# Layer 1's experts in a four-layer kernel: output pieces of 32 columns, the ranking inside the first expert, and mu loaded two tiles before its square

## The chip, the core and the metric

The kernel runs on one core of one Trainium2 chip. A core has a tensor engine (PE, with its weight loads shown apart as PEld), a vector engine (DVE), a scalar engine (ACT), a general engine (POOL) and a queue processor (SP) that issues most of the transfers between memory and the core's buffers. [...] The metric is device microseconds of one execution; the figure that counts is the median of several runs.

## The reference, cut to what matters

Four layers follow one another, each adding to the stream `x` of 32 x 64 = 2048 tokens of 512 numbers. The change lies in layer 1, a mixture of 32 experts, and in one preparation for layer 2 that is done meanwhile.

```python
# layer 1
logits = x @ gate_w.T + gate_b                    # 32 experts
topk_logits, topk_idx = top_k(logits, 4)
topk_weight = softmax(topk_logits)
order = argsort(topk_idx.reshape(-1))             # pairs of token and expert, by expert
xt = repeat(x, 4, axis=0)[order]
gate = ragged_dot(xt, w_gate, group_sizes) + b_gate[gid]
up = ragged_dot(xt, w_up, group_sizes) + b_up[gid]
gate = minimum(gate, 7); up = clip(up, -7, 7)
activated = (up + 1) * gate * sigmoid(1.702 * gate)
outs = ragged_dot(activated, w_down, group_sizes) + b_down[gid]
y = sum over a token's four outs, times topk_weight
# layer 2, the part prepared during layer 1
mu_n = mu / maximum(sqrt(sum(mu * mu, axis=0)), 1e-12)   # mu is 512 x 2048
```

## The kernel before

**Front of layer 1** (`layer1`, L1325). A loop over 16 tiles of 128 tokens adds layer 0's experts to the stream, mixes, computes the 32 logits and picks four experts per token. `put` (L845) and `placed` (L1167) give every pair of token and expert its place in the expert's list and write the token numbers into a small table `tok` of 96 x 128, a sum of products on PE. `end` (L1189) closes the front. First four small products bring the token numbers of the first two experts, which have fixed places, into a column form (`fixed`, L1192 to L1197), and a cast puts them into columns 0 to 4 of the integer table `stok` (L1198). Then comes the ranking of the other experts by load: totals (`tot`), keys, a permutation `perm`, the numbers of the ranked experts (`nth`), from which the gather addresses of their weights (`widx`) and biases (`each`) come, the lists in ranked order (`lists`, `ranked`), nine products that spread them over the 66 other tiles (L1225), a cast into the rest of `stok` (L1229), and the room of each expert (`room`, `count`). All of it stands ahead of the expert stage, and its constants, the group `cst1`, are loaded into a pool of the front (L1336).

**Expert stage** (`Moe.run`, L1011). The ranked experts have 320, 320, 352, 320 (three), 288 (15) and 256 (11) rows, end to end 9088 rows, 71 output tiles of 128. Three local functions issue the work of PE, whose order is written out by hand: `follow` (L1025) makes each PE instruction come after the one issued before it.

- `turn(t)` (L1035) transposes gathered rows `xr` of tile t and copies them to `xT`, by ACT and DVE in turn.
- `into(u, ic)` (L1050) multiplies the rows of expert u by half `ic` of its gate and up weights (`gu`, four PSUM buffers) and hands them to `l1_expert` (L712): DVE, a sigmoid on ACT into `sg`, a product on POOL (L722, kept in program order), and DVE again, into `hT`.
- `out_of(t)` (L1066) multiplies by the down weights into `y`. A tile can hold rows of two experts; `of_expert` lists its pieces (expert, column, row, count), which are at most 32 rows at row 32 or 96, at most 64 at row 64, and up to 128 at row 0. DVE adds the bias piece by piece into one of four `yo` buffers (L1079), and SP writes it out (L1082).

The loop at L1093 goes over experts and interleaves: after each of the four products of an expert comes a `turn` for the next expert and an `out_of` of the one before. POOL issues the gathers: `ready` (L891) asks for five tiles of rows right after `end`; in the first expert, `rows_to` and `weights` (L1113 to L1115) ask for tiles 5 to 7 and for the third expert's weights after the first half; later ones are asked for two experts ahead. The first two experts' weights are loaded by SP.

**Beside it.** After each `out_of`, `ahead` (L1383) is called. Every fourth of the first 16 tiles it computes slots; from tile 16 on it takes one step of the generator `layer2_ahead` (L1395): eleven loads of layer 2's weights, two steps of small work, and then, one a tile, 16 steps that each load 128 x 512 of mu (`mus`, two buffers) through SP and at once square and sum it on ACT (L1424 to L1428). A power on POOL (`cn`, L1429) and three DVE steps end it. `keep_in_program_order`, also as `pin`, holds an instruction at its place in its engine's order.

Of the kernel before, what the change touches and what calls it, by code (L numbers as in the profile page):

```python
# [47 lines left out]
CH = NK // 3  # L48


_GROUPS = ("cst", "cst01", "cst3", "cst1")


def _spread():

    sel, at = [], FIXED1 * 320 // P
    for shift in range(0, P, 32):
        for low in range(2 if shift else 1):
            s = np.zeros((P, TILES1 - at), np.float32)
            for u in range(FIXED1, E1):  # L60
                for c in range(-(-CAP1[u] // P)):
                    t = (BASE1[u] + c * P) // P + low
                    if BASE1[u] % P == shift and c * P + low * (P - shift) < CAP1[u]:
# [9 lines left out]
    s, parts = sel[0]  # L73
    odd = s * (np.arange(P)[:, None] % 2).astype(np.float32)
    return [(s - odd, parts), *sel[1:], (odd, parts)]


def _consts():
# [43 lines left out]
    d["spread"] = np.concatenate([s for s, _ in _spread()], 1)  # L122
    return dict(zip(_GROUPS, (a, b, c, d)))


def _rope_table():
# [99 lines left out]
class Prog:  # L226
# [9 lines left out]
        self.ident = self.c("ident")  # L236
        self.ones = self.c("ones")

    def constants(self, pool, group):
        t = self.load(pool, group)  # L240
# [471 lines left out]
def l1_expert(g, sb, hT, gate, up, bias):  # L712

    nc = g.nc
    ga = sb.tile([P, gate.shape[1]], F32, name="ga")
    nc.vector.tensor_scalar(ga, gate, bias[:, 0:1], 7.0, ALU.add, ALU.min)
    sg = sb.tile([P, gate.shape[1]], F32, name="sg")
    nc.scalar.activation(sg, ga, AF.Sigmoid, scale=1.702)  # L718
    up_ = sb.tile([P, gate.shape[1]], F32, name="up")
    nc.vector.tensor_scalar(up_, up, bias[:, 1:2], 7.0, ALU.add, ALU.min)  # L720
    nc.vector.tensor_scalar(up_, up_, -7.0, 1.0, ALU.max, ALU.add)
    g.pin(nc.gpsimd.tensor_tensor(ga, ga, sg, ALU.mult))  # L722
    nc.vector.tensor_tensor(hT, up_, ga, ALU.mult)  # L723


class Moe:
# [8 lines left out]
    def __init__(self, g, ctx, keep, E, K, caps, V, wname, wlen, act, scale, bias=None):  # L735
# [28 lines left out]
        for parts, sizes, whole in (  # L764
            (self.of_unit, [n for _, _, n in self.units], True), (self.of_expert, caps, False)
        ):
            at = 0
            for k, size in enumerate(sizes):
                col = 0
                while col < size:  # L770
                    row = at % P
                    n = min(size - col, P - row)
                    if not whole and row:
                        n = min(n, 64 if row == 64 else 32)
                    parts[at // P].append((k, col, row, n))
                    col, at = col + n, at + n

    def weights(self, e):
        if e < self.E and e not in self.wts:
# [118 lines left out]
    def rows_to(self, end):  # L898

        while self.asked < min(end, self.tiles):  # L900
            t = self.asked
            self.xrs[t] = self.xp.tile([P, D], F32, name="xr")
            self.g.gather(self.xrs[t], self.rows, self.stok[:, t : t + 1], later=self.ranked)
            self.asked += 1

    def beyond(self):

# [103 lines left out]
    def run(self, xs, per_tile):  # L1011
# [8 lines left out]
        with ExitStack() as ctx:  # L1020
# [45 lines left out]
            def out_of(t):  # L1066
                y = ps.tile([P, D], F32, name="y", tag="y")
                for ic in range(2):
                    for e, col, row, n in self.of_expert[t]:
                        wd = self.parts(self.weights(e))[2]  # L1070
                        follow(nc.tensor.matmul(  # L1071
                            y[row : row + n, :], hTs[e][:, ic, col : col + n], wd[:, ic, :],
# [17 lines left out]
            while turned < tiles_to(0):  # L1090
                turn(turned)
                turned += 1
            for u in range(len(self.units)):  # L1093
                k = 0
                e = self.units[u][0]
# [5 lines left out]
                for ic in range(2):  # L1101
                    for _ in into(u, ic):
                        if turned < tiles_to(u + 1):
                            turn(turned)
                            turned += 1
                        k += 1
                        if k > 1 and u and (done + 1) * P <= ends[u - 1]:
                            out_of(done)
                            done += 1
# [41 lines left out]
class Ranked(Moe):  # L1151
# [3 lines left out]
    def begin(self, sb, bank, at):  # L1155
        nc, g = self.g.nc, self.g
        self.bank, self.at = bank, at
        nc.vector.memset(self.pre[:, 0], 0.0)
        self.tok = sb.tile([TC1, P], F32, name="tokens1", bufs=1)
        nc.vector.memset(self.tok, 0.0)  # L1160
        self.number = sb.tile([32, P], F32, name="number1", bufs=1)
        nc.vector.tensor_scalar(self.number, g.ones[0:32, :], g.c("p")[0:32], None, ALU.mult)
        self.room = self.keep.tile([P, 2, E1], F32, name="room1")
        self.widx = self.keep.tile([P, E1], I32, name="widx1")
        self.each = self.keep.tile([P, E1], I32, name="each1")

    def placed(self, sb, hot, i, n):  # L1167

# [20 lines left out]
    def end(self, sb):  # L1189
# [3 lines left out]
        for o, cols, which in (  # L1193
# [1 line left out]
            (fixed[64:P, 2:5], slice(0, 64), slice(1, 96, 32)), (fixed[0:64, 3:5], slice(64, P), slice(1, 64, 32)),  # L1195
        ):
            nc.tensor.matmul(o, tok[:, cols], ident[0:TC1, which], start=True, stop=True)  # L1197
        nc.vector.tensor_copy(self.stok[:, 0:5], fixed)  # L1198

        tot = self.at[:, 0:E]  # L1200
        nc.tensor.matmul(tot, g.ones, self.pre[:, NT], start=True, stop=True)
        key = sb.tile([P, E], F32, name="key", bufs=1)
        nc.vector.tensor_tensor(key, tot, g.c("keym"), ALU.mult)
        nc.vector.tensor_tensor(key, key, g.c("keyc"), ALU.add)
        junk = sb.tile([P, E], F32, name="junk1", bufs=1)
        own = sb.tile([P, 2], F32, name="own1", bufs=1)
# [4 lines left out]
        perm = sb.tile([TC1, TC1], F32, name="perm1", bufs=1)  # L1211
        nc.vector.tensor_scalar(perm, g.c("blk")[0:TC1], own[0:TC1, 1:2], None, ALU.is_equal)
        nth = self.at[:, 32:64]
        nc.tensor.matmul(nth, self.number, perm[0:32, 0:32], start=True, stop=True)
        nc.vector.tensor_scalar(self.widx, nth, float(P), g.c("p"), ALU.mult, ALU.add)
        nc.vector.tensor_copy(self.each, nth)
        lists = self.bank[0:TC1, 256:384]
        nc.tensor.matmul(lists, perm, tok, start=True, stop=True)
        ranked = sb.tile([TC1, P], F32, name="ranked1", bufs=1)
        nc.vector.tensor_tensor(ranked, lists, g.c("within")[0:TC1], ALU.mult)  # L1220
        first, n = FIXED1 * 320 // P, self.tiles - FIXED1 * 320 // P
        table, at, k = self.bank[:, 384 : 384 + n], 0, 0
        todo = [(part, j) for j, (_, parts) in enumerate(_spread()) for part in parts]
        for k, ((to, row, rows), j) in enumerate(todo):
            nc.tensor.matmul(  # L1225
                table[to : to + rows], ranked[:, row : row + rows], g.c("spread")[0:TC1, j * n : (j + 1) * n],
                start=k == 0, stop=k == len(todo) - 1,
            )
        nc.vector.tensor_copy(self.stok[:, first:], table)  # L1229

        dg = sb.tile([32, 2, E], F32, name="dg1", bufs=1)
        for k, name in enumerate(("base1", "cap1")):
            nc.vector.scalar_tensor_tensor(
                junk[0:32], perm[0:32, 0:32], 1.0, g.c(name)[0:32], ALU.mult, ALU.mult, accum_out=own[0:32, k : k + 1]
            )
            nc.vector.tensor_scalar(dg[:, k], ident[0:32, 0:32], own[0:32, k : k + 1], None, ALU.mult)
        room = self.at[:, 64:128]
        nc.tensor.matmul(room, g.ones[0:32, :], dg.rearrange("p k e -> p (k e)"), start=True, stop=True)
# [86 lines left out]
def layer1(g, bridge, combined, beside, w2):  # L1325
    tc, nc, a = g.tc, g.nc, g.a
    with ExitStack() as ctx:
# [67 lines left out]
def layer2_ahead(g, w):  # L1395
# [25 lines left out]
    nc.vector.tensor_scalar(w["mask"], adf, g.c("pd16"), sc, ALU.is_equal, ALU.mult)  # L1421
    yield
    cs = pool.tile([P, 16], F32, name="cs2")
    for e in range(16):  # L1424
        m = sb.tile([P, D], F32, name="mus", bufs=2)
        g.dma(m, a["mu_s"][e * P : (e + 1) * P, :])
        nc.scalar.activation(m, m, AF.Square, accum_out=cs[:, e : e + 1])
# [1013 lines left out]
```

## Time and profile before

| what | us |
|---|---|
| median of 3 runs (lowest, highest) | 2646.71 (2644.03, 2647.79) |
| the profiled execution | 2657.32 |
| its span, first to last instruction | 2655.4 |
| DVE cast of the first five tiles' token numbers (L1198), start | 734.98 |
| first gather of the expert stage on POOL, start | 740.42 |
| first gu product on PE, start | 748.26 |
| last y product of the stage, start | 1179.3 |
| the 16 mu loads on SP, first and last issue | 941.9, 1045.1 |
| the 16 squares on ACT, each; first and last start | 0.63; 946.9, 1048.4 |

Times of instructions count from the start of the span. In a row of the timeline stand start, length, engine, line, operation, the tile written and those read, the shapes, a count of merged records, and in brackets how long the engine had been idle and what ended the idle time. "128*32 128x512" is a stationary operand of 128 rows and 32 columns with 512 columns streamed past it. An f32 product leaves two records. A row of the waits has the instruction that waited, what it waited for, the sum, the count and the longest.

### The profile page before, as it was taken

Reading aid. Unit: us, or ns where it says so; the run is one execution under the profiler, and the core shown is the slowest. Engines: PE = TensorE matmul, PEld = TensorE weight load, DVE = VectorE, ACT = ScalarE, POOL = GpSimd, SP = SyncE. Lnnn points to the kernel's source line nnn. Section 1 sums busy time; section 2 is a strip of 40 time slices with the busy share of each in tenths; the row PEclk is TensorE's granted clock in tenths of the full one; section 3 lists DMA queues with packets and bytes.
Section 4 is the critical chain, followed back from the end, with each engine's and each line's share of the span. In section 5 each row is a group of like instructions: output and inputs, shape, how many; then the busy total and the mean of one; then the engine's idle time right before and its main releaser. Section 6 shows DMA issues by size and latency. Waiting matters only on the chain.

```text
span 2655.4 us, 42159 instructions
## 1 busy us (share of the span) xinstructions
PE 2479.6 (93%) x16444; PEld 1626.1 (61%) x16459; DVE 1411.6 (53%) x3463; ACT 719.6 (27%) x1505; POOL 906.5 (34%) x955
## 2 busy tenths in 40 slices
PE   6999998997789999978999999999999999979998
PEld 4777775664556655756666666666666665445554
DVE  3666656653745444445554544454444432557886
ACT  2444330111311111101322222222222221246664
POOL 2222215533244434433333333333332311573440
PEclk9999998997689999999999999999999999989999
DMA  2333224456556866854222222222222313524441
GB/s 99 106 120 130 102 72 165 170 167 194 182 179 215 344 245 217 275 173 149 67 70 74 74 73 73 72 70 70 70 70 74 97 58 122 170 67 121 135 136 45
DMA packets 132421, 339.34 MB, mean 128 GB/s; under 512 B 23977, under 2 KB 24777, under 8 KB 124912
## 3 DMA queue, kind: packets, MB, share of 16 engines
q1 hardware_dynamic: 90576, 188.83, 20.7%
q0 software_dynamic: 41056, 141.89, 16.9%
q10 hardware_dynamic: 576, 5.77, 0.5%
q8 instruction: 135, 2.21, 0.3%
q14 instruction: 78, 0.64, 0.1%
HBM read 245.21 MB, written 107.22 MB: 133 GB/s over the span
## 4 chain that ended last, share of the span: by engine, by line
PE 41%; DVE 10%; issue 2%; POOL 1%; DMA 1%; ACT 0%; another core or an unknown queue 0%; ACTq 0%; POOLq 0%; SPq 0%; DVEq 0%
PE out L1814 9%; PE lp L1671 6%; PE gp L1803 3%; PE pp L2128 3%; PE zp L1748 3%; PE yp L1616 2%; PE y L2376 2%; PE hp L1780 2%; PE pT L2329 2%; PE op L2354 2%; PE sp L2307 2%; DVE xt L1145 1%; PE ep L1757 1%; DVE inv L1707 1%; PE kp L2280 1%
## 5 line engine op out<-in xcount | busy, mean ns | idle before, releaser
L1059 PE MATMUL gu<-xT,wt 128*128 128x320 f32 (+3 forms) x1472 | 398.9, 418 | 4.8 <-ACT xT L299 3.7
L1059 PEld LDWEIGHTS gu<-xT,wt 128*128 128x128 f32 x1472 | 277.5, 193 | 125.0 <-issue 52.8
L1814 PE MATMUL out<-sb_w,gT 128*128 128x512 f32 x512 | 233.5, 599 | 12.4 <-DVE nn L1651 6.6
L1671 PEld LDWEIGHTS lp<-xnT,sb_mu 128*128 128x128 f32 x2048 | 234.8, 193 | 9.2 <-issue 6.7
L1671 PE MATMUL lp<-xnT,sb_mu 128*128 128x128 f32 x2048 | 237.8, 276 | 2.1 <-DVE xnT L301 1.4
L1748 PE MATMUL zp<-sb_w,xnT 128*128 128x512 f32 x512 | 228.4, 595 | 5.6 <-DVE z L1750 5.5
L1071 PE MATMUL y<-wt,hT 128*128 128x512 f32 (+3 forms) x492 | 216.7, 596 | 2.3 <-DVE hT L723 2.3
L329 POOL DMA_INDIRECT kvst<-kv,gidx x96 | 97.0, 1010 | 280.9 <-DMA oldkv<-kvst 212.0
L1807 DVE COPY gT<-gp 128x512 f32<-128x512 f32 x64 | 44.3, 692 | 251.8 <-PE gp L1803 251.4
L1814 PEld LDWEIGHTS out<-sb_w,gT 128*128 128x128 f32 x512 | 93.2, 190 | 117.6 <-issue 95.2
L1748 PEld LDWEIGHTS zp<-sb_w,xnT 128*128 128x128 f32 x512 | 93.7, 190 | 113.4 <-issue 99.9
L329 POOL DMA_INDIRECT yk<-ys,slot x96 | 104.1, 1085 | 125.3 <-SPq L917 66.2
L329 POOL DMA_INDIRECT kvt<-newkv,oidx x96 | 99.8, 1040 | 134.9 <-DMA kvt<-oldkv 76.9
L329 POOL DMA_INDIRECT xr<-rows,stok x106 | 102.6, 968 | 81.1 <-DVE stok L1229 40.7
L1785 ACT ACTIVATE h<-hp 128x512 f32<-128x512 f32 x128 | 69.5, 595 | 218.5 <-PE hp L1780 218.3
L1071 PEld LDWEIGHTS y<-wt,hT 128*128 128x128 f32 (+3 forms) x492 | 75.4, 175 | 78.4 <-issue 62.9
L722 POOL TENSOR_TENSOR ga<-ga,sg 128x288 f32<-128x288 f32 (+3 forms) x64 | 50.5, 789 | 183.3 <-ACT sg L718 182.1
L1825 POOL TENSOR_TENSOR xt<-xt,bc_bias 128x512 f32<-128x512 f32 x16 | 20.5, 1280 | 228.5 <-DMA x<-xt 213.2
L1676 DVE TENSOR_TENSOR lT<-lp,cmu 128x512 f32<-128x512 f32 x64 | 43.5, 680 | 94.4 <-PE lp L1671 89.1
L1803 PEld LDWEIGHTS gp<-lT,h 128*64 128x64 f32 x2048 | 66.3, 140 | 38.7 <-issue 25.8
L1709 POOL TENSOR_TENSOR eT<-eT,inv 128x512 f32<-128x512 f32 x64 | 71.7, 1122 | 52.2 <-DVE inv L1708 43.9
L1079 DVE TENSOR_TENSOR yo<-y,bd 128x512 f32<-128x512 f32 (+3 forms) x88 | 60.7, 689 | 53.3 <-PE y L1071 52.0
(426 smaller groups left out, 4641.0 us busy)
## 6 DMA issues: line engine op xcount, KB each, us to landing
ys<-yo SPq DMA_DIRECT2D x106, 256.0 KB
oldkv<-kvst SPq DMA_DIRECT2D x96, 224.0 KB
kvt<-oldkv SPq DMA_DIRECT2D x96, 224.0 KB
ys<-zero SPq DMA_DIRECT2D x10, 2048.0 KB
xt<-x SPq DMA_DIRECT2D x62, 256.0 KB
x<-xt SPq DMA_DIRECT2D x48, 256.0 KB
wt<-w_e SPq DMA_DIRECT2D x7, 1536.0 KB
sb_w<-w SPq DMA_DIRECT2D x5, 1024.0 KB
```

Of the source, the lines that this page charges most:

```text
L329: ins = self.nc.gpsimd.indirect_dma_start(out=out, out_offset=None, in_=src, in_offset=bass.IndirectOffsetOnAxis(ap=idx, axis=0), **kw)
L1059: follow(nc.tensor.matmul(o, wj[:, c, ic * P : (ic + 1) * P], xTs[u][:, c, 0:n], start=c == 0, stop=c == 3))
L1071: follow(nc.tensor.matmul(y[row : row + n, :], hTs[e][:, ic, col : col + n], wd[:, ic, :], start=ic == 0, stop=ic == 1,))
L1079: nc.vector.tensor_tensor(yo[r], y[r], self.bds[e][r], ALU.add)
L1616: g.first(c, nc.tensor.matmul(yp, self.xT[:, c, :], w["w_2"][:, c, :], start=c == 0, stop=False))
L1671: g.first(e + c, nc.tensor.matmul(lp[:, e, :], w["mu"][:, c, (4 * q + e) * P : (4 * q + e + 1) * P], self.xnT[:, c, :], start=c == 0, stop ...
L1709: g.pin(nc.gpsimd.tensor_tensor(e3, e3, inv.unsqueeze(2).to_broadcast([P, 8, T]), ALU.mult))
L1748: g.first(c, nc.tensor.matmul(zp, self.xnT[:, c, :], w["w1"][:, c, cols], start=c == 0, stop=c == 3))
L1785: g.pin(nc.scalar.activation(self.hs[q][b], hp[:, b], AF.Gelu))
L1803: g.first(e + b + k, nc.tensor.matmul(gp[r, e, cols], self.hs[q][b][:, e, r], self.lT[q][:, e, cols], start=True, stop=True))
L1814: g.first(e, nc.tensor.matmul(self.out, self.gTs[q][:, e, :], w["w2"][:, 4 * q + e, :], start=q + e == 0, stop=q + e == 6 and q == 3))
L2128: nc.tensor.matmul(pp, xT[i][:, c, :], (w["w_kv3"] if z else wq)[:, c, :], start=c == 0, stop=c == 3)
```

## The change

1. `pieces` is a second list beside `of_expert`: where a tile has a piece whose count isn't a multiple of 64, all its pieces are cut into pieces of 32 rows. `out_of` multiplies by `pieces`; the bias is still added by `of_expert`.
2. `end` keeps the fixed products alone, and their cast goes into a table of its own, `fixed`. The ranking is the generator `rank`, in three parts, run by `next(ranking)` after the first expert's transposes and after its first and second product. Its constants are two groups now, `cst1` and `cst1s`, loaded by SP into `yo` buffers of the expert stage; a third `yo` buffer and one `y` bank are its working space. The even and odd split of the spreading products is gone (eight products), and one product with zeros (`none`) ends the sum, so nine remain.
3. The mu loop takes 18 iterations: the square of iteration e is of the load of iteration e - 2, and the first 16 iterations take two steps each.
4. `sg` in the experts' form has two buffers, not three.

```diff
@@ constants
+    def constants(self, pool, group, **kw):
+        if kw:
+            n = self.a[group].shape[1]
+            t = pool.tile([P, D], F32, **kw)
+            self.dma(t[:, 0:n], self.a[group], later=False)
+        else:
+            t = self.load(pool, group)
@@ l1_expert
-    sg = sb.tile([P, gate.shape[1]], F32, name="sg")
+    sg = sb.tile([P, gate.shape[1]], F32, name="sg", **(dict(bufs=2) if gate.shape[1] > P else {}))
@@ Moe
+        self.pieces = [
+            parts if all(n % 64 == 0 for *_, n in parts) else
+            [(e, col + k, row + k, 32) for e, col, row, n in parts for k in range(0, n, 32)]
+            for parts in self.of_expert
+        ]
...
-            self.g.gather(self.xrs[t], self.rows, self.stok[:, t : t + 1], later=self.ranked)
+            self.g.gather(self.xrs[t], self.rows, self.tokens_of(t), later=self.ranked)
@@ run
-                    for e, col, row, n in self.of_expert[t]:
+                    for e, col, row, n in self.pieces[t]:
...
+            ranking = self.rank(sb, ps, follow)
+            next(ranking, None)
             for u in range(len(self.units)):
...
                             turn(turned)
                             turned += 1
                         k += 1
+                        next(ranking, None)
                         if k > 1 and u and (done + 1) * P <= ends[u - 1]:
@@ Ranked
+        self.fixed = self.keep.tile([P, FIXED1 * 320 // P], I32, name="fixed1")
+
+    def tokens_of(self, t):
+        n = FIXED1 * 320 // P
+        return self.fixed[:, t : t + 1] if t < n else self.stok[:, t - n : t - n + 1]
...
-        nc.vector.tensor_copy(self.stok[:, 0:5], fixed)
...
+        nc.vector.tensor_copy(self.fixed, fixed)
+
+    def rank(self, sb, ps, follow):
+
+        g, nc, E, tok, ident = self.g, self.g.nc, self.E, self.tok, self.g.ident
+        for group in ("cst1", "cst1s"):
+            g.constants(sb, group, name="yo", bufs=4)
+        work = sb.tile([P, D], F32, name="yo", bufs=4)
...
+        follow(nc.tensor.matmul(tot, g.ones, self.pre[:, NT], start=True, stop=True))
+        g.pin(nc.vector.tensor_tensor(key, tot, g.c("keym"), ALU.mult))
         nc.vector.tensor_tensor(key, key, g.c("keyc"), ALU.add)
...
         nc.vector.tensor_scalar(perm, g.c("blk")[0:TC1], own[0:TC1, 1:2], None, ALU.is_equal)
+        nc.vector.tensor_scalar(number, g.ones[0:32, :], g.c("p")[0:32], None, ALU.mult)
+        yield
+
+        follow(nc.tensor.matmul(lists, perm, tok, start=True, stop=True))
+        follow(nc.tensor.matmul(nth, number, perm[0:32, 0:32], start=True, stop=True))
+        nc.vector.tensor_tensor(ranked, lists, g.c("within")[0:TC1], ALU.mult)
...
+        yield
+
+        todo = [(part, j) for j, (_, parts) in enumerate(_spread()) for part in parts]
+        for k, ((to, row, rows), j) in enumerate(todo):
+            follow(nc.tensor.matmul(
+                table[to : to + rows], ranked[:, row : row + rows], g.c("spread")[0:TC1, j * n : (j + 1) * n],
+                start=k == 0, stop=False,
+            ))
+        follow(nc.tensor.matmul(table, ranked, g.c("none")[0:TC1], start=False, stop=True))
+        nc.vector.tensor_copy(self.stok[:, 0:n], table)
+        follow(nc.tensor.matmul(room, g.ones[0:32, :], dg, start=True, stop=True))
         nc.vector.tensor_copy(self.room.rearrange("p k e -> p (k e)"), room)
...
@@ layer1
-            g.constants(wp, "cst1")
@@ layer2_ahead
-    for e in range(16):
-        m = sb.tile([P, D], F32, name="mus", bufs=2)
-        g.dma(m, a["mu_s"][e * P : (e + 1) * P, :])
-        nc.scalar.activation(m, m, AF.Square, accum_out=cs[:, e : e + 1])
+    mus = {}
+    for e in range(18):
+        if e >= 2:
+            m = mus.pop(e - 2)
+            nc.scalar.activation(m, m, AF.Square, accum_out=cs[:, e - 2 : e - 1])
+        if e < 16:
+            mus[e] = sb.tile([P, D], F32, name="mus", bufs=2)
+            g.dma(mus[e], a["mu_s"][e * P : (e + 1) * P, :])
         yield
+        if e < 16:
+            yield
```

More of the change, by code (lines that the diff above doesn't have):

```diff
@@ L48 @@
 CH = NK // 3
-_GROUPS = ("cst", "cst01", "cst3", "cst1")
+_GROUPS = ("cst", "cst01", "cst3", "cst1", "cst1s")
 def _spread():
@@ L72, in _spread @@
                 sel.append((s, parts))
-    s, parts = sel[0]
-    odd = s * (np.arange(P)[:, None] % 2).astype(np.float32)
-    return [(s - odd, parts), *sel[1:], (odd, parts)]
+    return sel
 def _consts():
@@ L121, in _consts @@
     d["within"] = (p[:, None] // 32 * P + p[None, :] < np.array(CAP1)[p % 32][:, None]).astype(f)
-    d["spread"] = np.concatenate([s for s, _ in _spread()], 1)
-    return dict(zip(_GROUPS, (a, b, c, d)))
+    d["none"] = np.zeros((P, TILES1 - FIXED1 * 320 // P), f)
+    s = {"spread": np.concatenate([s for s, _ in _spread()], 1)}
+    return dict(zip(_GROUPS, (a, b, c, d, s)))
 def _rope_table():
@@ L237, in __init__ @@
         self.ones = self.c("ones")
-    def constants(self, pool, group):
-        t = self.load(pool, group)
+    def constants(self, pool, group, **kw):
[5 more added lines that the diff above has]
+            t = self.load(pool, group)
         at = 0
@@ L902, in rows_to @@
             self.xrs[t] = self.xp.tile([P, D], F32, name="xr")
-            self.g.gather(self.xrs[t], self.rows, self.stok[:, t : t + 1], later=self.ranked)
+            self.g.gather(self.xrs[t], self.rows, self.tokens_of(t), later=self.ranked)
             self.asked += 1
+    def tokens_of(self, t):
+        return self.stok[:, t : t + 1]
+    def rank(self, sb, ps, follow):
+        return iter(())
     def beyond(self):
@@ L1158, in begin @@
         nc.vector.memset(self.pre[:, 0], 0.0)
-        self.tok = sb.tile([TC1, P], F32, name="tokens1", bufs=1)
+        self.tok = self.keep.tile([TC1, P], F32, name="tokens1")
         nc.vector.memset(self.tok, 0.0)
-        self.number = sb.tile([32, P], F32, name="number1", bufs=1)
-        nc.vector.tensor_scalar(self.number, g.ones[0:32, :], g.c("p")[0:32], None, ALU.mult)
         self.room = self.keep.tile([P, 2, E1], F32, name="room1")
@@ L1165, in begin, with tokens_of @@
         self.each = self.keep.tile([P, E1], I32, name="each1")
+        self.fixed = self.keep.tile([P, FIXED1 * 320 // P], I32, name="fixed1")
+    def tokens_of(self, t):
+        n = FIXED1 * 320 // P
+        return self.fixed[:, t : t + 1] if t < n else self.stok[:, t - n : t - n + 1]
     def placed(self, sb, hot, i, n):
@@ L1197, in end, with rank @@
             nc.tensor.matmul(o, tok[:, cols], ident[0:TC1, which], start=True, stop=True)
[L1198 to L1203, printed above, removed]
+        nc.vector.tensor_copy(self.fixed, fixed)
+    def rank(self, sb, ps, follow):
+        g, nc, E, tok, ident = self.g, self.g.nc, self.E, self.tok, self.g.ident
+        for group in ("cst1", "cst1s"):
+            g.constants(sb, group, name="yo", bufs=4)
+        work = sb.tile([P, D], F32, name="yo", bufs=4)
+        key, junk, own = work[:, 0:32], work[:, 32:64], work[:, 64:66]
+        perm, ranked = work[0:TC1, 96:192], work[0:TC1, 192:320]
+        dg, number = work[0:32, 320:384], work[0:32, 384:512]
+        bank = ps.tile([P, D], F32, name="y", tag="y")
+        tot, nth, room = bank[:, 0:32], bank[:, 32:64], bank[:, 64:128]
+        n = self.tiles - FIXED1 * 320 // P
+        lists, table = bank[0:TC1, 128:256], bank[:, 256 : 256 + n]
+        follow(nc.tensor.matmul(tot, g.ones, self.pre[:, NT], start=True, stop=True))
+        g.pin(nc.vector.tensor_tensor(key, tot, g.c("keym"), ALU.mult))
         nc.vector.tensor_tensor(key, key, g.c("keyc"), ALU.add)
-        junk = sb.tile([P, E], F32, name="junk1", bufs=1)
-        own = sb.tile([P, 2], F32, name="own1", bufs=1)
         nc.vector.scalar_tensor_tensor(junk, key, 1.0, g.c("same32"), ALU.mult, ALU.mult, accum_out=own[:, 0:1])
@@ L1210, in end @@
         )
-        perm = sb.tile([TC1, TC1], F32, name="perm1", bufs=1)
         nc.vector.tensor_scalar(perm, g.c("blk")[0:TC1], own[0:TC1, 1:2], None, ALU.is_equal)
-        nth = self.at[:, 32:64]
-        nc.tensor.matmul(nth, self.number, perm[0:32, 0:32], start=True, stop=True)
+        nc.vector.tensor_scalar(number, g.ones[0:32, :], g.c("p")[0:32], None, ALU.mult)
[3 more added lines that the diff above has]
+        nc.vector.tensor_tensor(ranked, lists, g.c("within")[0:TC1], ALU.mult)
         nc.vector.tensor_scalar(self.widx, nth, float(P), g.c("p"), ALU.mult, ALU.add)
         nc.vector.tensor_copy(self.each, nth)
[L1217 to L1231, printed above, removed]
         for k, name in enumerate(("base1", "cap1")):
@@ L1235, in end @@
             )
-            nc.vector.tensor_scalar(dg[:, k], ident[0:32, 0:32], own[0:32, k : k + 1], None, ALU.mult)
-        room = self.at[:, 64:128]
-        nc.tensor.matmul(room, g.ones[0:32, :], dg.rearrange("p k e -> p (k e)"), start=True, stop=True)
+            nc.vector.tensor_scalar(dg[:, 32 * k : 32 * k + 32], ident[0:32, 0:32], own[0:32, k : k + 1], None, ALU.mult)
+        yield
[8 more added lines that the diff above has]
+        follow(nc.tensor.matmul(room, g.ones[0:32, :], dg, start=True, stop=True))
         nc.vector.tensor_copy(self.room.rearrange("p k e -> p (k e)"), room)
```

## The prediction, made before the result was known

> **What bounds the kernel now.** I read the page's busy times first, then the table of engine time by stage, then the timeline of TensorE (PE) inside the stage that the change touches, and last the waits there.
>
> ```profile
> PE 2479.6 (93%) x16444; PEld 1626.1 (61%) x16459; DVE 1411.6 (53%) x3463; ACT 719.6 (27%) x1505; POOL 906.5 (34%) x955
> ```
>
> ```profile
> 690.00:770.00 80.00, 61.92 (x261) 43.25 (x262) 42.80 (x141) 18.72 (x32) 20.70 (x18) 0.65 0.46 159
> 770.00:1190.00 420.00, 402.58 (x1570) 261.56 (x1568) 197.96 (x394) 54.28 (x131) 170.17 (x183) 0.98 0.69 245
> ```
>
> The columns are stretch, length, then busy time of PE, weight loads, DVE, ACT and POOL, then granted clock, DMA share and GB/s. Layer 1's expert stage (770 to 1190) is bound by PE, 402.6 of 420.0 us. Ahead of it (690 to 770) PE has idle time and a clock of 0.65: that stretch is bound by a chain.
>
> The timeline of PE inside the stage shows what a shared tile costs:
>
> ```profile
> 778.94 1.94 PE L1071 MATMUL y<-wt,hT 128*64 128x512 f32 x8
> 780.81 2.42 PE L1059 MATMUL gu<-xT,wt 128*128 128x320 f32 x8
> 783.06 1.88 PE L1071 MATMUL y<-wt,hT 128*128 128x512 f32 x4
> 784.78 2.32 PE L1059 MATMUL gu<-xT,wt 128*128 128x320 f32 x8
> 835.55 4.00 PE L1071 MATMUL y<-wt,hT 128*96 128x512 f32 x8
> 839.48 2.42 PE L1059 MATMUL gu<-xT,wt 128*128 128x320 f32 x8
> 905.28 4.04 PE L1071 MATMUL y<-wt,hT 128*32 128x512 f32 x12
> 909.25 2.21 PE L1059 MATMUL gu<-xT,wt 128*128 128x288 f32 x8
> 1399.10 1.08 PE L1767 MATMUL csum<-lT,sb_cst 128*32 128x128 f32 x32
> 1400.11 1.16 PE L1780 MATMUL hp<-z,ew 64*128 64x128 f32 x16
> ```
>
> Each row is start, length, form and count; every f32 product leaves two records. From start to next start, a whole tile takes 784.78 - 783.06 = 1.72 us for four rounds (2 halves of the hidden width, 2 passes), 0.43 a round. A tile shared 64+64 takes 1.87 for eight records: the halves run side by side. A tile shared 96+32 takes 3.93, one shared 32+32+64 takes 3.97: as long as eight rounds one after the other (3.44) and 0.5 more. The last pair is a step of layer 2 that already writes four 32-column pieces side by side: 32 records in 1.01 us, where 32 rounds of 128 columns (0.43/4 = 0.107) in a row would be 3.4.
>
> The waits of PE in the stage, then the rows around the longest:
>
> ```profile
> PE gu L1059 <- ACT xT L299: 3.7, 1, 3.7
> PE y L1071 <- DVE hT L723: 2.3, 2, 1.7
> PE tp L1038 <- ACT xT L299: 1.3, 1, 1.3
> ```
>
> ```profile
> 1016.09 0.63 ACT L1427 ACTIVATE mus<-mus 128x512 f32<-128x512 f32 x1 [3.88 <-DMA mus<-mu_s]
> 1016.72 0.46 ACT L299 COPY xT<-tp 128x384 f32<-128x384 f32 x1
> 1017.23 4.21 PE L1059 MATMUL gu<-xT,wt 128*128 128x288 f32 x8 [3.67 <-ACT xT L299]
> ```
>
> ACT stands at the square of a mu tile that has not landed; the copy PE needs is queued behind it. After the gap PE's eight products take 4.00 us, not 1.94.
>
> Ahead of the stage the timeline has the ranking:
>
> ```profile
> 734.98 0.17 DVE L1198 CAST stok<-tok 128x5 int32<-128x5 f32 x1 [1.05 <-PE tok L1197]
> 736.61 3.54 PE L1225 MATMUL tok<-sb_cst,ranked 96*128 96x66 f32 x18 [0.38 <-DVE ranked L1220]
> 740.19 0.23 DVE L1229 CAST stok<-tok 128x66 int32<-128x66 f32 x1 [3.54 <-PE tok L1225]
> 740.42 0.94 POOL L329 DMA_INDIRECT xr<-rows,stok  x1 [40.71 <-DVE stok L1229]
> 748.26 4.07 PE L1059 MATMUL gu<-xT,wt 128*128 128x320 f32 x7 [0.56 <-issue]
> ```
>
> The token numbers of the first five tiles are ready at 735.15, but the first gather starts at 740.42, when the whole table is written, and the first expert 7.84 later.
>
> **What the Trainium skill says.** TensorEngine Tiling (Array Packing), Key Properties: column tiles load and multiply independently, but changing the tiling mode drains the array. The trace agrees: 64+64 costs 0.15 over a whole tile, mixed forms 2.2. TensorE: Matmul & The Clock Gate, Part 3 (Measured speedup): three 32-column tiles of 512 gave 2.38x, so overlap need not be perfect; the csum row here gives 3.4 / 1.01 = 3.4x of four. The same page, Part 1: the array runs at half clock until it has been busy for a window of about 3.4 us. The trace agrees: at 748.26 and 1017.23 PE needs some 4 us to get to full speed.
>
> **The pieces.** From the capacities, 8 of 71 tiles hold a piece not a multiple of 64: five 96+32 (tiles 12, 19, 28, 37, 46), three 32+32+64 (24, 33, 42). Before: 5 x 3.93 + 3 x 3.97 = 31.6 us. After: four pieces of 32 in one mode, so four rounds of 0.43 and the 0.15 that both 64+64 and csum show over their rounds (1.01 - 8 x 0.107): 1.87. Eight make 15.0. Gain **16.6 us**, all on PE's path. Bounds: no overhead, 8 x 1.72, gain 17.8; an overlap of only 2.38/3, 16 x 0.43 / 3.17 = 2.17 a tile, gain 14.2. The adds of L1079 are not split; DVE is busy 198 of 420 us, so they hide.
>
> **mu two tiles ahead.** Same loads and squares, but each load is issued two iterations, four output tiles, before its square; the last iterations move from about tile 45 to tile 62. ACT waited 58.7 us for mu in the stage, at most 7.7 at once; four tiles are some 20 us, so the data is there. PE's three stalls: at 1017, 3.84 late, then 4.00 against 1.94, 0.85 against 0.44, 2.36 against 1.94 at the low clock, 6.7 in all; at 979.6 to 981.0, 1.5; at 1054.4 to 1056.1, 1.8, where POOL's product `ga` stood behind the power `cn`, which waited for the last square. Sum 10.0. The 2.94 us power stays on POOL, now without that wait; I leave 0.5 for it. Gain **9.5**. Bounds 6 (if the clock-loss stall leaves and another comes) and 10.5. SP's mu issue waits for the square just ahead of it, and behind it on SP stand writes of finished tiles; four `yo` buffers cover some 20 us. If that cover failed, each wait would cost up to 5.3, the one wait of this kind in the trace.
>
> **The ranking.** It leaves the chain: 740.42 - 735.15 = 5.3, and 0.3 for the DVE steps of L1208 between the last token updates: 5.6 earlier. It comes back on PE inside the first expert, in PE's fixed order: `tot` 0.64, nearly hidden in the 0.56 that PE waits for its first copy (0.1 counted); `lists` and `nth` 0.74 + 0.63 at half clock; the table 3.54 (nine products again); `room` 0.69. The first eight products (4.4 us) warm the clock, so I halve these: 0.7 + 1.8 + 0.35. Sum 3.0; net gain **2.6**. Bounds: gain 5.6 if it falls in other waits; loss of 3 if everything stays at half clock (5.7) and DVE's pinned `key` waits about 3 for the constants. These constants are two loads of about 0.23 MB on SP; DMA is idle from 730 to 740 (0 GB/s), and SP has nothing before the first output at 768, which hides them. Behind `key` on DVE stand the first `ga` steps, for which ACT, POOL and through PSUM the PE wait; PE has four `gu` buffers, so it can write the second half of the first unit before it needs them. On POOL, gathers of tiles 5 to 7 and of expert 2's weights wait for the table, about 753.5 by this sum against an issue at 755.04 now, behind the same `ga`. Expert 2's weights landed at 768.1 and were used at 773.7: 5.6 spare, some 3 after the shift. Next late: the xr copy of tile 5, about 1.5 spare.
>
> **The rest, at nothing.** `sg` with two buffers: ACT waits only if POOL is two products behind; POOL is busy 170 of 420 us; lost cover costs 0.9 a product. The constants' earlier load at about 593 goes, where PE does not wait for DMA. Weights in the stage land 5 to 13 us before use, so a PE 6% faster does not meet them.
>
> **Sum.** 16.6 + 9.5 + 2.6 = 28.7. Against the profiled execution (2657.3, its span 2655.4 and 1.9 around it) 2628.6. That execution is 10.6 over the median of the runs, 2646.7; nothing in the sum scales with this, so I forecast **2618**.
>
> **Rivals.**
> - The pieces overlap only in pairs, as 64+64 does: eight rounds, 3.6 a tile, gain 2.8. For: no row shows four streams of 512. Against: csum. 2632, chance 0.06.
> - The ranking inside the expert costs 3 (bounds above), through the half clock or late gathers: 28.7 - 5.6 = 23.1, 2624. For: POOL and DVE now queue behind the table. Chance 0.18.
> - The mu wait moves (to SP, or to the weight gathers) and 3 of 9.5 stay gained: 2625. Against: 20 us of lead. Chance 0.06.
> - Slower: four pieces run one after the other, 16 x 0.43 + 0.15 = 7.0 a tile, 24.6 lost on PE in these 8 tiles against 12.1 gained elsewhere: 2659. It decides from 5.5 us a tile ((31.6 + 12.1) / 8). Against it speak csum and 64+64. Chance 0.03.
>
> The forecast has 0.67. **Range** 2611 (gains 17.8, 10.5, 5.6 are 33.9: 2612.8, less 2 for the spread of the runs) to 2630, which takes in the second and third rival. A measurement here can tell about 0.2%, 5 us. Faster 0.96, same 0.01, slower 0.03.
>
> **What would show it.** Right: eight L1071 groups of 16 records 128*32 at about 1.9 us to the next start; no wait of ACT for mu, none of PE over 1 us after 800; the first xr gather some 0.2 after the cast of `fixed`, PE's first gu about 5 earlier, and the stage from first gu to last y about 23 shorter. Wrong: groups near 3.6 or 7; an idle PE at the first turn of tile 5 or at expert 2; DVE or SP waiting for constants.

## The result and the profile after

| | before | after |
|---|---|---|
| median (lowest, highest), 4 runs each | 2647.25 (2644.03, 2649.08) | 2618.81 (2617.31, 2622.33) |
| profiled execution, its span | 2657.32, 2655.4 | 2617.31, 2615.5 |
| last product of the front's loop (`mm`) to first gu, PE | 35.5 | 30.1 |
| of this, to the first gather | 27.7 | 22.0 |
| first gu to the end of the last y, PE | 431.6 | 412.4 |
| ACT's wait for mu, sum and longest (before: at 15 squares; 6.8 at the other one is put down to a gather) | 58.7, 7.7 | 106.4, 11.8 |

The ratio is 0.9896, 95% interval 0.9879 to 0.9913: 28.4 us less, between 23 and 32. Forecast were 28.7 less. That the totals meet is in part luck, and it hides that one term of the sum failed: in the two profiled executions the stretch from the last `mm` to the last y, which holds all that was changed, is 24.6 us shorter, not 28.7. The other 15.3 us between the spans lie where nothing was changed (ahead of and in the loop of layer 1's front, and behind the last y); the execution profiled of before was 10 over its median, and such parts differ by several us between the profiles here (the front's loop alone: 62.2 to 70.2 us in ten other profiles).

The table of engine time by stage for the changed kernel, in two stretches that lie as far from the first gu and the last y as those of before. Columns as there: stretch, length, busy time of PE, weight loads, DVE, ACT, POOL, then clock, DMA share, GB/s.

```profile
673.00:753.00 80.00, 57.63 (x294) 41.39 (x293) 51.70 (x162) 22.41 (x39) 28.90 (x20) 0.74 0.48 165
753.00:1154.00 401.00, 386.07 (x1633) 259.01 (x1632) 196.62 (x395) 53.51 (x131) 169.55 (x184) 0.99 0.74 260
```

The stage lost 19 us of length and PE 16.5 of its busy time (402.58 to 386.07): nearly the price of the pieces by itself. It is still PE that sets its length.

The shared tile of 96+32 that had 4.00 us and 3.93 to the next start, in the timeline of PE after:

```profile
821.00 1.92 PE L1086 MATMUL y<-wt,hT 128*32 128x512 f32 x16
822.86 2.42 PE L1074 MATMUL gu<-xT,wt 128*128 128x320 f32 x8
```

Sixteen records now, eight before, and 1.86 us to the next start. The other seven groups of this form take 1.85 or 1.86.

The ranking, in the timeline of the first expert (all engines, cut to the rows concerned):

```profile
722.75 0.17 DVE L1219 CAST fixed<-tok 128x5 int32<-128x5 f32 x1 [1.20 <-PE tok L1218]
723.18 0.95 POOL L333 DMA_INDIRECT xr<-rows,fixed  x1 [29.51 <-DVE yo L1243]
...
731.28 3.58 PE L1074 MATMUL gu<-xT,wt 128*128 128x320 f32 x8 [0.29 <-issue]
...
738.47 1.87 PE L1260 MATMUL y<-yo 96*128 96x66 f32 x16
740.18 0.39 PE L1264 MATMUL y<-yo 96*128 96x66 f32 x2
```

The first gather starts 0.26 after the cast of the first five tiles' numbers has ended; before it was 5.3. (Its row names as what it waited for the next step of DVE, L1243, which ends 0.09 before it.) The nine spreading products, 3.54 us in the front at a granted clock of 0.50, take 2.1 at 1.00 inside the expert. No row of the stage shows PE waiting at tile 5 or at the third expert's weights.

The waits in the stage, of PE and then of ACT for mu:

```profile
PE y L1086 <- DVE yo L1094: 2.2, 1, 2.2
PE gu L1074 <- ACT xT L303: 1.9, 2, 1.2
PE y L1086 <- DVE hT L727: 0.6, 1, 0.6
```

```profile
ACT mus L1455 <- DMA mus<-mu_s: 106.4, 16, 11.8
```

Here the prediction's mu term is wrong. ACT waits for mu longer than before, at every one of the 16 squares, and PE still has two of the waits over 1 us that were to be gone. The timeline around the longer one shows the order in which it came about (SPq is SP's queue):

```profile
1012.52 0.39 SPq L262 DMA_DIRECT2D mus<-mu_s  x1
...
1020.93 0.63 ACT L1455 ACTIVATE mus<-mus 128x512 f32<-128x512 f32 x1 [8.91 <-DMA mus<-mu_s]
...
1021.56 0.56 ACT L303 COPY xT<-tp 128x512 f32<-128x512 f32 x1
1022.02 0.41 ACT L722 ACTIVATE sg<-ga 128x256 f32<-128x256 f32 x1
...
1025.17 1.95 PE L1086 MATMUL y<-wt,hT 128*128 128x512 f32 x4 [2.16 <-DVE yo L1094]
```

ACT stood at the square from 1020.93 - 8.91 = 1012.02, which is 0.5 us before SP issued the load of that very tile. The source puts two iterations between load and square. In the program that ran, the square stands close behind the load: at 15 of the 16, ACT has nothing or one sigmoid between the issue of a load and its square, and at the other one (the load at 974.30) the square before it and one sigmoid. Behind the square stood a copy for PE and the sigmoid that POOL's product waits for; through POOL, DVE's `hT` and its add into `yo`, PE lost 2.16 us.

### The profile page after: what moved, and what is told of

The parts are those of the page before. It is cut to its first block, busy times and chain, and to the rows that moved or that the text cites. A ratio compares the mean times of both kernels' runs of the same rounds, so it can differ in the third digit from the quotient of the medians.

```text
span 2615.5 us, 42259 instructions
## 1 busy us (share of the span) xinstructions
PE 2443.5 (93%) x16496; PEld 1608.8 (62%) x16511; DVE 1409.0 (54%) x3463; ACT 718.9 (27%) x1505; POOL 910.5 (35%) x955
## 4 chain that ended last, share of the span: by engine, by line
PE 56%; DVE 10%; DMA 4%; issue 3%; POOL 1%; ACT 1%; another core or an unknown queue 0%; SPq 0%; ACTq 0%; POOLq 0%; DVEq 0%
PE out L1847 9%; PE gu L1074 7%; PE lp L1704 7%; PE y L1086 3%; PE gp L1836 3%; PE pp L2161 3%; PE zp L1781 3%; PE yp L1649 2%; PE y L2409 2%; PE hp L1813 2%; PE op L2387 2%; PE pT L2362 2%; PE sp L2340 2%; DMA xr<-rows,stok 2%; DVE xt L1163 1%
## 5 line engine op out<-in xcount | busy, mean ns | idle before, releaser
L1086 PE MATMUL y<-wt,hT 128*128 128x512 f32 (+2 forms) x544 | 199.9, 595 | 2.7 <-DVE yo L1094 2.2
L1086 PEld LDWEIGHTS y<-wt,hT 128*128 128x128 f32 (+2 forms) x544 | 72.8, 166 | 65.1 <-issue 52.1
L1733 ACT ACTIVATE eT<-eT 128x512 f32<-128x512 f32 x64 | 40.3, 630 | 177.4 <-DVE eT L1730 159.7
```

The source lines that it names most:

```text
L1086: follow(nc.tensor.matmul(y[row : row + n, :], hTs[e][:, ic, col : col + n], wd[:, ic, :], start=ic == 0, stop=ic == 1,))
```

## The experiments

Two readings of these traces were to be told apart. **Theory:** the three parts save PE what the prediction said, and the mu part falls short because the squares, which nothing holds in program order, slip ahead in ACT's queue. **Rivals:** the rest of PE's waits has another cause (POOL's power, SP's writes); or a part is worth nothing and its place in the sum is taken by another.

Gains below are against the kernel before on the same chip. There were three such chips, and its median on them was 2608.1 to 2609.9 us. It is shorter than in the first measurement because of the work behind the expert stage: what follows the last y took the changed kernel 1471.8 us there and 1438.8 on one of the three. Intervals are 95%. "Front" is the last `mm` to the first gu, "stage" the first gu to the end of the last y, both from the profile; the kernel before has 35.5 and 431.6.

### One part alone

The pieces alone, `pieces` being made as in the change:

```diff
-                    for e, col, row, n in self.of_expert[t]:
+                    for e, col, row, n in self.pieces[t]:
```

> The kernel before with the pieces of 32 columns alone. Theory (four column tiles run side by side, the sum's term 16.6 us): each of the eight shared tiles takes 1.86 us to the next start instead of 3.93 or 3.97, the stage from first gu to last y shortens by 16 to 17 us, the time falls by 14 to 17 us (some of it can be eaten by the three stalls at mu, which stay). Rival (part of the gain seen in the whole change came from elsewhere, and the pieces only overlap in pairs): 3.6 us a tile, 3 us in all.

The mu loop alone:

```diff
-    for e in range(16):
-        m = sb.tile([P, D], F32, name="mus", bufs=2)
-        g.dma(m, a["mu_s"][e * P : (e + 1) * P, :])
-        nc.scalar.activation(m, m, AF.Square, accum_out=cs[:, e : e + 1])
+    for e in range(18):
+        if e >= 2:
+            m = mus.pop(e - 2)
+            nc.scalar.activation(m, m, AF.Square, accum_out=cs[:, e - 2 : e - 1])
...
```

> The kernel before with the mu loop of the change alone. Theory A (the prediction: a lead of four tiles takes ACT's wait away): ACT's waits for mu under 10 us in total, PE's stalls in the stage under 1 us each, gain 9 to 10 us. Theory B (formed from the trace of the changed kernel, where ACT still waited 106 us in total for mu and loads led their squares by 3 to 11 us only: the squares are not held in program order and are put ahead in ACT's queue): ACT still waits about 100 us in total, PE keeps stalls of 3 to 4 us in sum, gain 4 to 7 us, because the loads are rarer, not because they lead.

The ranking alone, with the two buffers of `sg`: everything of the change but these two parts.

```diff
-        nc.vector.tensor_copy(self.stok[:, 0:5], fixed)
+        nc.vector.tensor_copy(self.fixed, fixed)
+
+    def rank(self, sb, ps, follow):
...
+            ranking = self.rank(sb, ps, follow)
+            next(ranking, None)
```

> The kernel before with the ranking inside the first expert, the own table of the fixed two, and two buffers of sg alone. Theory: the first gather starts 5 to 6 us after less work between the last mm product and it (27.7 us before, 22 after), the ranking's products cost PE 2.2 to 3 us inside the first expert, gain 2.5 to 3.5 us. Rival (the front's 12 us of earlier first gather in the changed kernel's trace belong to the change): gain 10 us or more.

| alone | ratio | gain, us | front | stage |
|---|---|---|---|---|
| pieces | 0.9968 (0.9955 to 0.9980) | 8.3 (5.2 to 11.7) | 35.4 | 425.4 |
| mu | 0.9963 (0.9950 to 0.9977) | 9.6 (6.0 to 13.0) | 35.5 | 422.4 |
| ranking | 0.9999 (0.9987 to 1.0012) | 0.3 (-3.1 to 3.4) | 30.3 | 435.1 |

Laid product by product against before, the **pieces** save 1.98 to 2.12 us at each of the eight tiles, 16.3 in all, but the stage is only 6.2 shorter. PE, now faster, waits more for ACT and for what hangs on it. Its waits in that run's stage (before: 3.7, 2.3 and 1.3):

```profile
PE y L1076 <- DVE hT L723: 5.8, 2, 5.2
PE gu L1064 <- ACT xT L299: 4.2, 1, 4.2
PE tp L1043 <- ACT xT L299: 3.0, 1, 3.0
PE y L1076 <- DVE yo L1084: 1.7, 1, 1.7
```

and the two rows of its timeline that belong to the longest:

```profile
1032.68 2.94 POOL L353 TENSOR_TENSOR cn<-cs,sb_cst 128x16 f32<-128x16 f32 x1 [6.05 <-ACT mus L1432]
...
1039.60 1.91 PE L1076 MATMUL y<-wt,hT 128*32 128x512 f32 x2 [5.19 <-DVE hT L723]
```

So the 16.3 were there, and 10 of them were given back to the mu squares and to the power that waits for the last of them. The expectation's warning that the stalls can eat some of the gain came true; its 16 to 17 us of stage and 14 to 17 of time did not.

**Mu** alone shortens the stage by 9.2 us: PE's three stalls are gone (no wait over 0.6 is left), as the prediction's 9.5 had it. Yet ACT waits for mu longer than the 58.7 us of before:

```profile
ACT mus L1428 <- DMA mus<-mu_s: 86.5, 15, 10.4
```

So neither theory holds as a whole: ACT's waits are those of B, PE's stalls and the gain those of A. What stood behind ACT's waits, copies among it, was not yet due on PE. With PE at another pace, in the changed kernel, some of it was.

The **ranking** alone brings the front 5.2 us and costs the stage 3.5: 2.5 in the first expert, 1.0 at PE's stalls for mu, which fell differently. The time does not show the 1.7 that remains; the 2.5 to 3.5 us that were expected lie at the upper edge of its interval.

### Squares held in program order

```diff
-            nc.scalar.activation(m, m, AF.Square, accum_out=cs[:, e - 2 : e - 1])
+            g.pin(nc.scalar.activation(m, m, AF.Square, accum_out=cs[:, e - 2 : e - 1]))
```

This one line in the changed kernel:

> The changed kernel with the sixteen squares of mu held at their place in program order on ACT, nothing else. Theory B (the squares were put ahead): each load now leads its square by four tiles, some 18 us, ACT's waits for mu fall from 106 us to under 20, PE's stalls of 1.2, 2.2 and 0.7 us in the second half of the stage go, and it is 3 to 4 us faster than the changed kernel (2614 to 2616, gain to the kernel before 32 to 34 us). Rival (the residual stalls come from elsewhere, such as the output adds on DVE): no difference to the changed kernel, 28 us to the kernel before.

and the same kernel a second time, with the changed kernel itself beside it on one chip:

> The changed kernel with the squares of mu held in program order, beside the changed kernel on the same chip. Theory (the squares slip ahead in ACT's queue, so the lead is lost): 4 to 6 us less than the changed kernel, about -32 against the kernel before, stage 408, ACT's wait for mu below 3 us in all against 106. Rival (the rest of PE's waits has another cause, POOL or the writes): the same time as the changed kernel within 1 us, though ACT's wait is gone.

> The changed kernel once more, beside its parts on one chip. Against the kernel before about -27 us (it was -28 in its own measurement). In the stage from the first gu to the last y, 412 us with some 5 us of waits of PE for mu left in it.

| | ratio | gain, us | front | stage |
|---|---|---|---|---|
| changed kernel | 0.9887 (0.9869 to 0.9904) | 29.5 (25.1 to 34.2) | 30.0 | 415.7 |
| squares held, first | 0.9870 (0.9847 to 0.9893) | 33.9 (27.9 to 39.9) | 30.0 | 407.8 |
| squares held, second | 0.9862 (0.9843 to 0.9882) | 36.0 (30.8 to 41.0) | 29.9 | 407.8 |

ACT's wait for mu with the squares held and the longest wait of PE behind the first gu (both from the first of the two runs), and the rows of the timeline that answer to those above:

```profile
ACT mus L1455 <- DMA mus<-mu_s: 1.2, 1, 1.2
PE y L1086 <- DVE hT L727: 0.6, 1, 0.6
```

```profile
1007.77 0.44 SPq L262 DMA_DIRECT2D mus<-mu_s  x1
...
1024.01 0.59 ACT L303 COPY xT<-tp 128x512 f32<-128x512 f32 x1 [6.33 <-PE tp L1053]
1024.49 0.63 ACT L1455 ACTIVATE mus<-mus 128x512 f32<-128x512 f32 x1
```

The load issued at 1007.77 is squared at 1024.49, 16.7 us later, without a wait and behind the copy that PE needs. The lead is 7.6 to 19.8 us over the 16 tiles, mostly 16 to 18; without the pin it was 2.8 to 11.3. In both, SP issues the loads and the writes in the same order. PE has no wait over 0.6 us left in the stage, so the theory holds, and POOL's power and SP's writes, which are still there, cost PE nothing by themselves. The stage is 4.6 us shorter than that of the changed kernel in its first profile, 7.9 than in the second, whose waits fell worse. This version is faster than both kernels: 2573.8 against 2580.1 us for the changed one, on one chip. The intervals of the two gains overlap, but no run of the one reaches one of the other (at most 2575.4 us against at least 2576.9, four runs each), and their stages don't meet either (407.8 twice against 412.4 and 415.7).

The kernel before with mu two iterations ahead and held, and nothing else (the mu loop above, with the line of the pin):

> The kernel before with mu two iterations ahead and its squares held in program order, nothing else. Theory (a wait of ACT costs only where the copy that PE needs next is queued behind it): ACT's wait for mu falls from 87 us (run of mu alone) to below 3, but PE's three stalls were gone there already, so the time is that of mu alone: -9 to -10 us against the kernel before, stage 421 to 422.5. Rival (ACT's waits cost by their sum): clearly more, -15 or beyond.

Ratio 0.9956 (0.9943 to 0.9969), gain 11.5 us (8.1 to 14.9), stage 421.2, ACT's wait for mu 0.2 us. Taking 86 us of ACT's waits away brings the stage 1.2 us over mu alone: here the sum of an engine's waits was no measure of their price.

### All but the ranking, and the ranking's two halves

The pieces and mu with its squares held, the ranking left where it was (the two edits above and the pin, on the kernel before):

> Pieces and mu with the squares held in program order, the ranking as before (ahead of the experts, one table). Theory: pieces 16.3 and mu 9.5 now add up, so -26 us against the kernel before, stage about 405.5; and 3.5 us slower than the changed kernel with pinned squares, since the ranking's move is worth 5.7 in the front less 2.2 in the first expert. Rival (the ranking's move is worth nothing, as its run alone had it): within 1 us of that kernel. Rival (pieces and mu still take from each other): -20 or less.

The same, with the own table in addition:

```diff
-        nc.vector.tensor_copy(self.stok[:, 0:5], fixed)
+        nc.vector.tensor_copy(self.fixed, fixed)
...
-            self.g.gather(self.xrs[t], self.rows, self.stok[:, t : t + 1], later=self.ranked)
+            self.g.gather(self.xrs[t], self.rows, self.tokens_of(t), later=self.ranked)
```

> As the run without the ranking's move, but the first five tiles have their own table `fixed`; the ranking's arithmetic stays ahead of the experts. Theory: the first gather comes 5.2 us earlier, and PE's table of 3.5 us then lies beside the gather's latency, so that only some 1.5 us of it stays: PE's first gu 3.7 us earlier, nothing added in the first expert, so 3.7 us faster than without it and equal to the changed kernel with pinned squares within 1 us. Rival (the table must leave the front to gain anything): no gain over the run without it.

| | ratio | gain, us | front | stage |
|---|---|---|---|---|
| without the ranking's move | 0.9891 (0.9873 to 0.9908) | 28.4 (24.0 to 33.1) | 35.1 | 405.0 |
| own table alone | 0.9889 (0.9874 to 0.9905) | 29.0 (24.8 to 32.9) | 35.4 | 405.4 |

The first run is the clearest of all: the stage is 26.6 us shorter, 16.3 in the eight tiles, 10.1 at PE's three stalls and 0.2 in the first expert, and 26.1 were predicted for the two parts. Apart they gave 6.2 and 9.2. Against it, the changed kernel with held squares has a front shorter by 5.1 to 5.2 and a stage longer by 2.8, all of it in the first expert (so `sg`, which has three buffers in the one and two in the other, costs nothing later): the ranking's move is worth 2.3 to 2.4 us of the trace. The medians on one chip, 2582.4 and 2573.8, differ by more than that, but with intervals of some 4 us each they neither confirm nor refute it.

The own table alone did nothing, as the rival had it, but the theory was not put to the test: the gather did not come earlier. Two rows of its timeline:

```profile
732.72 0.23 DVE L1241 CAST stok<-tok 128x66 int32<-128x66 f32 x1 [3.54 <-PE tok L1237]
732.96 0.94 POOL L329 DMA_INDIRECT xr<-rows,fixed  x1 [37.33 <-DVE stok L1241]
```

The gather reads `fixed`, ready since 727.69, and still starts when the cast of the whole table ends. Its rows go to buffers that are opened as the front's are given back, and the ranking works in those; that this is what it waits for is a guess that no run tested. So how much of the 5.2 could be had without moving the ranking stays open.

### Must neighbours differ in column group?

The prediction's slower rival let the four pieces run one after the other. The pieces alone, but with the loops turned, so that the four records of one 32-column group follow one another:

```diff
-                for ic in range(2):
-                    for e, col, row, n in self.pieces[t]:
+                for e, col, row, n in self.pieces[t]:
+                    for ic in range(2):
```

> The kernel before with the pieces alone, but both halves of the hidden width of one piece are issued before the next piece, so that the four records of one 32-column group follow one another. If the overlap needs neighbours in different groups (the slower rival of the prediction): 5.5 to 7 us a shared tile against 1.86, so 13 to 25 us slower than the kernel before. If a group's queue lets the next group start while it works: 1.9 a tile, as in the run of the pieces alone, -8 us. Between the two: 2 to 4 us a tile, near the 3.95 of before and so no change within 5 us.

Ratio 0.9965 (0.9953 to 0.9978), gain 9.1 us (5.7 to 12.3), stage 425.4 as with the pieces alone. In the timeline:

```profile
824.69 1.94 PE L1076 MATMUL y<-wt,hT 128*32 128x512 f32 x16
826.56 2.42 PE L1064 MATMUL gu<-xT,wt 128*128 128x320 f32 x8
```

1.87 us to the next start, as in the other order. The overlap is there in both of these orders, so the rival has no ground.

## Why the prediction came out as it did

- **Pieces: right.** 16.6 predicted, 16.3 measured (1.86 us a tile against 1.87; what stands ahead of five of the tiles took 0.1 longer). The slower rival and that of pairs are out. What the term left out is that a stall elsewhere can eat it: alone, 10 of 16.3 were eaten.
- **Mu: the step that failed.** It is the one that said "four tiles are some 20 us, so the data is there". It took the order of the source for the order in ACT's queue. A load's place was kept (SP's order did not change when the squares were held), a square's was not: it went to close behind its load, and ACT waited 106 us instead of none. The size of the stalls was right: 10.1 are gone once the squares are held, for 10.0 listed and 9.5 taken. Of these the changed kernel has 10.1 - 4.6 = 5.5 in one profile and 10.1 - 7.9 = 2.2 in another. The third rival had that end of it, "the mu wait moves", but looked for it on SP or in the gathers; it had not moved, it stayed on ACT. The chance of 0.06 was too low: nothing in the profile of before showed that a square stays where the source has it, and this one has no pin, where others have one.
- **Ranking: right in the traces, in both halves.** 5.6 earlier predicted, 5.1 to 5.7 measured. The cost in the first expert was put at 3.0 and is 2.3 (changed kernel against before) to 2.8 (against the kernel without the move). In the changed kernel it is `lists` and `nth` 0.65, the table 2.1, a wait of 0.3 and `room` 0.36, less the 1.0 by which the first eight gu products are faster (3.4 to the next start, 4.4 before): the granted clock over them was 0.65, and 0.50 before. Net that is 2.3 to 2.4 against the kernel without the move and 3.1 against before, for 2.6. No measured time is sharp enough to show it. The covers held: DVE's `key` did not wait for the constants (731.10, right behind a copy), the table was written at 740.84, 9.6 after the first gu, where the sum had it some 10.8 after, and nothing waited at tile 5.
- **The sum.** The parts were added as if independent. They are not, as long as stalls for mu are left: separately the stage gives 6.2 + 9.2 - 3.5 = 11.9, the changed kernel 19.2, and with the squares held 23.8, for 23.1 predicted. Front and stage together are then 29.3 us shorter, against 28.7 of the forecast: it described the change with each square at its place in the source, not as it ran.
- **The time.** 2618.8 for 2618, and this closeness is luck. With 24.6 us of gain in the changed stretch, about 4 of the measured 28.4 come from elsewhere or from chance; the interval (23 to 32) takes in both figures. The changed kernel's second measurement, 29.5 with 21.4 in the trace, leaves 8. Where they come from is open. The one part outside the stretch that leans the right way, the first gu of layer 0, starts at 419.1 to 423.2 in the five profiles with the ranking moved and at 419.9 to 425.6 in the seven without it. The means are 421.1 and 424.0, but the two groups overlap, so this is not shown.

In two places what the Trainium skill states was borne out: TensorEngine Tiling (Array Packing), Theoretical Speedup, gives up to 4x for 32 columns, and 16 rounds of 0.43 in 1.86 us are 3.7x. Its PSUM — Partial Sum Buffer, Engine vs sequencer instructions, has ACT's queue as strict first in, first out. The trace agrees: a square waited 8.91 us at 1020.93, and the copy and the sigmoid behind it ran only then. It fixes the order in which instructions run, but not that they were put into the queue in the order of the source.

## What to carry to other kernels

A load issued early helps only if its consumer stays late: look in the trace for where the consumer stands in its engine's queue, and hold it there if the tool that orders the instructions may move it. A stall that another engine sets takes back what is saved on the bound engine, so remove it first, or in the same step: here two parts gave 15.4 us of the stage apart and 26.6 together. A long sum of waits on an engine that is not the bound is no price (86 us of ACT's waits cost 1.2 of the stage here, and 106 us in another kernel 4.6); what counts is what is queued behind the wait, and whether the bound engine is due for it.

## What was not expected of the hardware

- Four 32-column groups of 512 columns overlap 3.7-fold (1.86 us for 16 records), and as well when four records of one group come in a row (1.87). A mix of widths (96+32, 32+32+64) took 3.93 and 3.97 us, no less than its eight rounds one after the other (3.44) and 0.5 more.
- A wait of PE near 4 us costs its clock, as the prediction had read at 1017.23, but not always as much: eight gu products of 288 columns, a record of 2.2 us as a rule, took 4.21 after 3.67 us idle (before), 3.04 after 3.61 (ranking alone) and 3.73 after 4.15 (pieces alone, 997.5 to 1001.6). The granted clock in these stretches was 0.50, 0.70 and 0.59. After the 2.16 us of the changed kernel it was 1.00, and the next eight products, of 256 columns, took their usual 1.89.
